# An RWKV block with routed experts on one core: the stages of time and channel mixing interleaved by batch

## The chip, the core and the metric

The kernel runs on one core of a Trainium2 chip, in fp32 throughout. Its time is the device time of one execution in microseconds (us); the figure that counts is the median of the runs shown. Five engines work side by side, each through its own list of instructions in a fixed order: TensorE (PE in the profile, with its weight loads PEld beside it), VectorE (DVE), ScalarE (ACT), GpSimd (POOL) and SyncE (SP), which issues the DMAs.

## The reference, cut to what matters

Four batches of 512 tokens with 512 channels pass through a modulated layer norm, a time mix, a channel mix, and then a block of two shared and sixteen routed experts (two of them for each token). Only the first part of it is touched. Cut down, with `h` the modulated layer norm of `x`:

```python
h1 = layer_norm(h, ln1_g, ln1_b); hh = time_shift(h1)     # one token back
k = (h1*tm_mk + hh*(1-tm_mk)) @ Wk.T                      # v and r alike
e2 = exp(tm_first + k - p); e1 = exp(-1e38 - p)           # p = max(-1e38, tm_first + k)
wkv = (e1*0 + e2*v) / (e1*0 + e2)
h = h + sigmoid(r) * wkv @ Wo.T                           # time mix
h2 = layer_norm(h, ln2_g, ln2_b); hh = time_shift(h2)
kk = (h2*cm_mk + hh*(1-cm_mk)) @ Wkey.T                   # 512 -> 2048
sr = sigmoid((h2*cm_mr + hh*(1-cm_mr)) @ Wcr.T)
h = h + sr * (silu(kk) @ Wval.T)                          # channel mix, 2048 -> 512
x = x + ga * h                                            # then the experts
```

Nothing passes from one batch to another before the experts, so the batches may be worked off in any order. The experts need the router's picks of all batches: the rows of each expert are counted batch by batch.

## The kernel before, in words

**Stages.** The work is a row of stages, one batch in each: T0 T1 T2 T3 (time mixes of batches 0 to 3), then C0 C1 C2 C3 (channel mixes), then the shared and routed experts. T0 (`time_first`, L402) starts the kernel and is of its own form.

**Time mix** (`time_mix`, L455). For each of four blocks of 128 output channels, m = 0 to 3, TensorE makes a k product, a v product and an r product (`k_step` L371, `v_step` L379, `r_step` L387), each a group of four 128x512 matmuls in `project` (L320). Behind each, VectorE, ScalarE and GpSimd work: after k the tiles p, e1, e2 (`exponents`, L338); after v the sum and the numerator av (`fraction`, L350); after r an exponential (`gated`, L358). What is left of a block, `divide` (L363), is put off: it is kept in a list `pend`, and `flush` (L334) issues it, at the next k or v step, or ahead of the output products. `divide` is one two-input VectorE operation, a reciprocal, and a GpSimd product that gives the finished gated tile. `o_steps(b)` (L393) flushes, then makes the output product of the time mix for each of four token tiles, four matmuls each (the last of the four needs the gated tile of m = 3), and VectorE adds the result onto the residual `x1s[b]`. In T2 and T3 the output products of the batch before are issued behind m = 0.

**Channel mix** (`channel_mix`, L577). First four products cr, one for each token tile (L596 to L614), with four sets of two subtractions on VectorE beside them (`key_terms`, L588; T1, T3, T2, T4 in the program's names). In C0 the output products of T3 stand behind the second cr. Then the key phase: four pairs of blocks, each with seven products of 128x256 matmuls (a Strassen form on 2x2 blocks; the banks are kx, ky and kz, and VectorE and ScalarE turn them into the tiles a11, a12, a21, a22; `ku` at L675 is VectorE's sum that releases ky's bank for its second use). Then the value phase: seven products in two halves each (`product`, L696; banks x, y, z), between which VectorE forms differences of the a tiles (`minus`, L720) and adds results to the residual (`result`, L723).

Strassen needs sums of weight blocks. Those for the keys are made in C0 by VectorE (`key_sums`, L504) and stored to DRAM for the later stages (`keep_keys`, L511). Those for the values (`value_sums`, L531) are made in T3: eight loads of quarters, sixteen subtractions of 128x512 on VectorE in four sets, and sixteen stores.

**What is woven in.** Each stage is a generator that yields behind each group of products, and at each yield `weave` (L1213) takes one step of a second generator, `back`. A list `plan` can say otherwise for each yield (0 or 1 steps):

```python
for _ in main:
    for _ in range(next(plan, 1)):
        next(back, None)
```

What is left of `back` when the stage's products are all issued is then drained. The back generators are the layer norms and the mixes ahead of a later stage, and the router behind an earlier one:

- `time_front(b)` (L272): statistics, modulation, statistics again, normed rows (ScalarE), then transposes on TensorE and the mixes for k, v and r. A statistics is `bn_stats`, `bn_aggr` and a small add on VectorE and a power on GpSimd; a modulation is two operations on VectorE.
- `channel_front(b)` (L305): statistics, normed rows, transposes, two mixes.
- `channel_back(b)` (L801): statistics, a modulated tile `h3r`, transposes, then the router: logits, the two picks, counts, and 8 small matmuls `ps_rows` at the end.

Before, T1 carries `time_front(2)`, T2 `time_front(3)`, T3 `front_and_sums` (L565: `channel_front(0)` with `value_sums` in its odd steps); C1 carries `channel_front(2)` and then `channel_back(0)`, C2 `channel_front(3)` and then `channel_back(1)`, C3 `channel_back(2)`; C0 carries `channel_front(1)`.

**Order and buffers.** The order of instructions on each engine is the order in which the program issues them (L66); no scheduler moves them. An instruction that must wait holds up all that stand behind it on its engine. All loads and stores of this part are issued on SP's queue, in the same way. Weights live in `wpool`: eight buffers of 1 MB, taken in turn, so that a load waits for the last reader of the tile that had its buffer (L72, L88). The time weights wk, wv, wr, wo are loaded once at the start (L113, L115); wcr and the first keys at T3 (L1273, L1274); then two tiles of keys for each pair (`load_keys`, L485) and seven tiles of values (`get`, L618) in each C stage. Rows of tokens live in 65 tiles of 128x512, and there are four `ps` and four `acc` banks of PSUM.

Of the kernel before, what the change touches and what calls it, by code (L numbers as in the profile page):

```python
# [44 lines left out]
def adaln_block(  # L45
# [274 lines left out]
    def project(w, acts, m, ps):  # L320

        for k in range(NK):
            nc.tensor.matmul(ps, w[:, k, m * P : (m + 1) * P], acts[k], start=(k == 0), stop=(k == NK - 1))  # L323

    def project_tokens(w, acts, t, ps):

        for k in range(NK):
            nc.tensor.matmul(ps, acts[k][:, t * P : (t + 1) * P], w[:, k, :], start=(k == 0), stop=(k == NK - 1))  # L328


    rws = [None] * B
    pend = []

# [36 lines left out]

    def k_step(b, m):  # L371
        ps = bank(f"ps_k_{b}_{m}")
        project(wk, time_mixes[b][MK], m, ps)
        yield
        out = exponents(b, m, ps)
        flush()
        return out

    def v_step(b, m, st, tag="ps"):  # L379
        ps = bank(f"ps_v_{b}_{m}", tag)  # L380
        project(wv, time_mixes[b][MV], m, ps)
        yield
        out = fraction(b, m, ps, *st)
        flush()
        return out

    def r_step(b, m, st):  # L387
        ps = bank(f"ps_r_{b}_{m}")
        project(wr, time_mixes[b][MR], m, ps)
        yield  # L390
        gated(b, m, ps, *st)

    def o_steps(b):  # L393
        flush()
        for t in range(NT):
            ps = bank(f"ps_o_{b}_{t}", "acc")
            project_tokens(wo, rws[b], t, ps)
            yield
            nc.vector.tensor_add(x1s[b][t], x1s[b][t], ps)
        rws[b] = None  # L400
# [53 lines left out]

    def time_mix(b):  # L455
        rws[b] = []
        if 1 < b < B - 1:
            time_loads(b + 1)
        for m in range(NK):
            st = yield from k_step(b, m)  # L460
            st = yield from v_step(b, m, st)
            yield from r_step(b, m, st)
            if m == 0 and b > 1:
                yield from o_steps(b - 1)
        time_mixes[b] = None


    h3_d = dram.tile([N, H], F32, tag="h3_d", name="h3_d")
# [33 lines left out]
    loaded = {}  # L502
# [28 lines left out]
    def value_sums():  # L531


        def load(n):
            t = [row_tile(f"wsum_{n}_{q}", (P, 2, HT)) for q in range(4)]
            for q in range(4):
                i, j = divmod(q, 2)
                at = i * (FF // 2) + n * 2 * P
                rows = wval_t[at : at + 2 * P, j * HT : (j + 1) * HT]
                nc.sync.dma_start(t[q], rows.rearrange("(k p) o -> p k o", p=P))  # L540
            return t

        def store(n, t):
            at = slice(n * 2 * HT, (n + 1) * 2 * HT)
            for i, q in ((T1, Q11), (T3, Q12), (T2, Q22), (T4, Q21)):
                nc.sync.dma_start(sums_d[i - T1, :, at].rearrange("p (k o) -> p k o", k=2), t[q])

        ahead = [load(0), load(1)]
        done = None
        yield  # L550
        for n in range(N_PAIR):
            t = ahead.pop(0)
            nc.vector.tensor_sub(t[Q11], t[Q12], t[Q11])
            nc.vector.tensor_sub(t[Q12], t[Q22], t[Q12])
# [10 lines left out]
    def front_and_sums():  # L565

        sums = value_sums()
        next(sums)
        for i, _ in enumerate(channel_front(0, "acc")):
            if i % 2:  # L570
                next(sums, None)
            yield
        yield from sums

    gas = {}

    def channel_mix(b):  # L577
# [18 lines left out]
        for t in range(NT):  # L596
            ps = bank(f"ps_cr_{b}_{t}")
            project_tokens(wcr, xr, t, ps)
            yield
            sr = row_tile(f"sr_{b}_{t}")  # L600
            nc.scalar.activation(sr, ps, AF.Sigmoid)
            nc.gpsimd.tensor_mul(sr, sr, ga)
            srs.append(sr)
            if b == 0 and t == 1:
                yield from o_steps(B - 1)
                key_sums(0)
            key_terms(t)
# [148 lines left out]
        result(2, HT, c5)  # L756

        if b + 1 < B:
            load_keys(b + 1, 0)
            gas[b + 1] = spread(GA, b + 1)  # L760
        yield from product(Q22, a12, Z, False)
        nc.vector.tensor_add(u2, u2, Z)
        result(0, HT, u2)

        yield from product(T4, a22, Y, False)
        nc.vector.tensor_add(c1, c1, Y)
        result(2, 0, c1)
# [445 lines left out]
    def weave(main, back, plan=()):  # L1213

        plan = iter(plan)
# [4 lines that stand above are left out]
    def drain(back):  # L1220
        for _ in back:
            pass

    def chained(*parts):
        for p in parts:
            yield from p()
# [39 lines left out]
        next(back)  # L1266
    weave(first, back, (1, 1, 1, 1, 0, 0, 0))
    drain(back)
    for b in range(1, B):
        if b + 1 < B:  # L1270
            back = chained(lambda: time_front(b + 1))
        else:
            wcr = load_w(wcr_t, "wcr")  # L1273
            loaded[0] = load_keys(0, 0)  # L1274
            back = front_and_sums()
            gas[0] = spread(GA, 0)
        weave(time_mix(b), back)
        drain(back)
    nc.sync.dma_start(router[:, :, :E_RT], w_router.rearrange("(k p) e -> p k e", p=P))
    for b in range(B):  # L1280
        parts = []
        if b + 1 < B:
            parts.append(lambda: channel_front(b + 1, "ps"))
        if b >= 1:
            parts.append(lambda: channel_back(b - 1))
        back = chained(*parts)

        plan = {0: [1] * 6 + [0] * 14, B - 1: [1] * 4 + [0, 0, 1] * 4}
        weave(channel_mix(b), back, plan.get(b, ()))
        drain(back)  # L1290
        if b == 0:
            clear_rest()
    shared = [load_shared(e) for e in range(E_SH)]
    gbs = [spread(GB, b) for b in range(B)]
    mids = [None] * B
# [87 lines left out]
```

## Time and profile before

| | |
|---|---|
| median of 3 runs | 1048.02 us (1046.33 to 1049.45) |
| the profiled execution, on its own clock | 1048.66 us |
| span of its trace | 1046.9 us |
| mean granted TensorE clock | 0.991 |
| start and end of T1 on TensorE | 96.74 to 139.69 us |
| T2 | to 205.15 us |
| T3 | to 267.19 us |
| C0, C1, C2 | to 394.73, 513.44 and 632.76 us |
| moved by DMA | 182.8 MB |

The span is what the trace covers; the execution's time is 1.8 us longer. Busy times count the instructions of an engine; weight loads (PEld) run beside the matmuls. In a line of a timeline the first number is the start in us of the span, the second the length, then engine, source line, operation, output and inputs by the program's names, and in brackets how long the engine was idle ahead of it and which instruction ended that wait.

### The profile page before, as it was taken

Reading aid. Unit: us, or ns where it says so; the run is one execution under the profiler, and the core shown is the slowest. Engines: PE = TensorE matmul, PEld = TensorE weight load, DVE = VectorE, ACT = ScalarE, POOL = GpSimd, SP = SyncE. Lnnn points to the kernel's source line nnn. Section 1 sums busy time; section 2 is a strip of 40 time slices with the busy share of each in tenths; the row PEclk is TensorE's granted clock in tenths of the full one; section 3 lists DMA queues with packets and bytes.
Section 4 is the critical chain, followed back from the end, with each engine's and each line's share of the span. In section 5 each row is a group of like instructions: output and inputs, shape, how many; then the busy total and the mean of one; then the engine's idle time right before and its main releaser. Section 6 shows DMA issues by size and latency. Waiting matters only on the chain. (4 is left out here: it accounts for less than half of the span.)

```text
span 1046.9 us, 11349 instructions
## 1 busy us (share of the span) xinstructions
PE 1013.1 (97%) x3824; PEld 667.1 (64%) x3824; DVE 637.5 (61%) x1174; ACT 302.2 (29%) x490; POOL 341.4 (33%) x322
## 2 busy tenths in 40 slices
PE   7998989989999999999999999999998999999997
PEld 2443434434478886888788886888745666566643
DVE  5887998897756535665757487447646322234427
ACT  1744452624323402621143102230030222122210
POOL 2453463532463007330164006420004222041250
PEclk9999989999999999999999999999999999999999
DMA  9700130443047761356332814642443999899853
GB/s 322 242 1 2 40 101 0 131 139 125 19 173 270 280 241 66 106 204 228 111 101 75 296 41 170 239 164 81 151 152 110 326 382 383 287 331 319 283 178 114
DMA packets 96619, 182.80 MB, mean 175 GB/s; under 512 B 7512, under 2 KB 50008, under 8 KB 92464
## 3 DMA queue, kind: packets, MB, share of 16 engines
q1 hardware_dynamic: 90720, 162.92, 45.0%
q0 software_dynamic: 5840, 19.14, 5.7%
q8 instruction: 31, 0.51, 0.2%
q14 instruction: 28, 0.23, 0.1%
HBM read 149.75 MB, written 32.29 MB: 174 GB/s over the span
## 5 line engine op out<-in xcount | busy, mean ns | idle before, releaser
L202 POOL TENSOR_TENSOR rstd_ln<-rstd_ln,minus_half 128x1 f32<-128x1 f32 x64 | 42.5, 664 | 192.0 <-DVE rstd_ln L201 179.5
L705 PE MATMUL ps_y<-wval,a 128*128 128x256 f32 x384 | 85.7, 380 | 0.0
L1112 POOL DMA_INDIRECT xg<-h_d,token x41 | 39.0, 950 | 126.0 <-PE ps_down L1151 41.1
L1151 PE MATMUL ps_down<-wrt,at 128*128 128x512 f32 x164 | 77.3, 593 | 1.7 <-issue 1.7
L705 PEld LDWEIGHTS ps_y<-wval,a 128*128 128x128 f32 x384 | 72.3, 190 | 9.5
L1135 PE MATMUL ps_up<-wrt,xt 128*128 128x256 f32 x328 | 77.8, 380 | 0.1
L246 DVE SCALAR_TENSOR_TENSOR mix_ln<-hT_ln,inv,mix_ln 128x511 f32<-128x511 f32 x64 | 56.4, 924 | 17.5 <-ACT mix_ln L240 16.8
L1135 PEld LDWEIGHTS ps_up<-wrt,xt 128*128 128x128 f32 x328 | 59.1, 190 | 7.5 <-DVE xt L1129 1.1
L634 PE MATMUL ps_ky<-T,keys_hi 128*128 128x256 f32 x256 | 60.9, 381 | 2.4 <-DVE ku L675 1.3
L1129 DVE COPY xt<-ps_xt 128x512 f32<-128x512 f32 x41 | 28.3, 689 | 55.8 <-PE ps_xt L1127 42.3
L328 PE MATMUL ps_o<-wo,av 128*128 128x512 f32 x128 | 57.9, 604 | 4.2 <-POOL av L366 4.0
L634 PE MATMUL ps_kx<-mix_ln,keys_lo 128*128 128x256 f32 x256 | 60.5, 379 | 0.0
L323 PE MATMUL ps_v<-mix_ln,wv 128*128 128x512 f32 x128 | 58.8, 603 | 0.0
L323 PE MATMUL ps_r<-mix_ln,wr 128*128 128x512 f32 x128 | 57.6, 593 | 0.1
L705 PE MATMUL ps_x<-wval,a 128*128 128x256 f32 x256 | 57.4, 380 | 0.0
L705 PE MATMUL ps_z<-wval,a 128*128 128x256 f32 x256 | 57.3, 380 | 0.0
L1057 PE MATMUL ps_up_sh<-h,wsh 128*128 128x512 f32 x128 | 57.2, 593 | 0.0
L1071 PE MATMUL ps_down_sh<-wsh,mid 128*128 128x512 f32 x128 | 56.3, 594 | 0.3 <-PEq L1325 0.3
L328 PE MATMUL ps_cr<-wcr,mix_ln 128*128 128x512 f32 x128 | 55.7, 592 | 0.0
L634 PEld LDWEIGHTS ps_ky<-T,keys_hi 128*128 128x128 f32 x256 | 47.9, 190 | 10.5 <-DVE ku L675 2.4
L222 ACT ACTIVATE xn_ln<-x,nm_ln,rstd_ln 128x512 f32<-128x512 f32 x32 | 25.8, 812 | 99.6 <-DVE nm_ln L215 99.5
L365 DVE RECIPROCAL p<-p 128x512 f32<-128x512 f32 x16 | 53.6, 3353 | 0.6
(223 smaller groups left out, 1834.9 us busy)
## 6 DMA issues: line engine op xcount, KB each, us to landing
wrt<-in_rt_up_dram SPq DMA_DIRECT2D x41, 512.0 KB
wrt<-in_rt_down_dram SPq DMA_DIRECT2D x41, 512.0 KB
wval<-sums_d SPq DMA_DIRECT2D x16, 1024.0 KB
wval<-in_wval_t_dram SPq DMA_DIRECT2D x12, 1024.0 KB
keys_lo<-keys_d SPq DMA_DIRECT2D x12, 1024.0 KB
y_d<-y SPq DMA_DIRECT2D x41, 256.0 KB
keys_hi<-keys_d SPq DMA_DIRECT2D x12, 768.0 KB
mod<-mod_d SPq DMA_DIRECT2D x22, 256.0 KB
```

The lines of the kernel that those rows point to most:

```text
L202: nc.gpsimd.tensor_tensor(rstd, rstd, minus_half, ALU.pow)
L246: nc.vector.scalar_tensor_tensor(t[:, 1:], hT[:, : T - 1], inv[:, m - MK, k : k + 1], t[:, 1:], ALU.mult, ALU.add)
L323: nc.tensor.matmul(ps, w[:, k, m * P : (m + 1) * P], acts[k], start=(k == 0), stop=(k == NK - 1))
L328: nc.tensor.matmul(ps, acts[k][:, t * P : (t + 1) * P], w[:, k, :], start=(k == 0), stop=(k == NK - 1))
L365: nc.vector.reciprocal(p, p)
L634: nc.tensor.matmul(ps[:, c * HT : (c + 1) * HT], w[:, k, c * P : (c + 1) * P], acts[k], start=(fresh and c == 0 and k == 0), stop=(c == 1 ...
L705: nc.tensor.matmul(ps[:, j * HT : (j + 1) * HT], acts[p][:, c, j * P : (j + 1) * P], w[:, i, :], start=(fresh and i == 0 and j == 0), stop ...
L1057: nc.tensor.matmul(ps, wu[:, k, m * P : (m + 1) * P], h3s[b][k], start=(k == 0), stop=(k == NK - 1))
L1071: nc.tensor.matmul(ps, mids[b][j][:, t * P : (t + 1) * P], shared[j // ND][1][:, j % ND, :], start=(j == 0), stop=(j == len(mids[b]) - 1),)
L1112: nc.gpsimd.indirect_dma_start(out=xg, out_offset=None, in_=h3_d, in_offset=bass.IndirectOffsetOnAxis(ap=token[:, s : s + 1], axis=0),)
L1135: nc.tensor.matmul(ps[:, :D], xt[:, k, :], wu[:, k, :], start=(k == 0), stop=(k == NK - 1))
L1151: nc.tensor.matmul(ps, at[:, j, :], wd[:, j, :], start=(j == 0), stop=(j == ND - 1))
```

## The change

The stages are put in the order T0 T1 C0 T2 C1 T3 C2 C3. What follows from that, and is part of it:

- The back generators move. T1, T2 and T3 now carry `channel_front(0)`, `channel_front(1)` and `channel_front(2)`. C0 carries the rest of `value_sums` and then `time_front(2)`; C1 `time_front(3)` and then `channel_back(0)`; C2 `channel_back(1)` and then `channel_front(3)`; C3 `channel_back(2)`. `front_and_sums` is gone; the first loads of `value_sums` are issued behind T1, its sixteen subtractions in C0's first yields.
- The output products of batch b+1 are issued in C(b), behind its second cr product, for b = 0, 1, 2. T2 and T3 have none any more.
- The time weights lose their buffers to keys and values, and are loaded again: wk, wv and wr late in C0 and C1 (ahead of the value products Q22 and T4), wo in T2 and T3 behind m = 0. That is eight loads of 1 MB more. The first keys of C1 and C2 are loaded behind m = 2 of T2 and T3, and no longer late in C0 and C1.
- wcr and the first keys are loaded ahead of T1, the rows of batch 3 (`time_loads(3)`) behind C0.

The number of matmuls and of operations on the data is the same.

```diff
+    tw = dict(k=wk, v=wv, r=wr, o=wo)
+    tw_next = {}
+
+    def load_time(*names):
+        for n in names:
+            tw_next[n] = load_w(dict(k=wk_t, v=wv_t, r=wr_t, o=wo_t)[n], f"w{n}")
...
     def time_mix(b):
         rws[b] = []
-        if 1 < b < B - 1:
-            time_loads(b + 1)
+        tw.update(tw_next)
+        tw_next.clear()
         for m in range(NK):
             st = yield from k_step(b, m)
             st = yield from v_step(b, m, st)
             yield from r_step(b, m, st)
-            if m == 0 and b > 1:
-                yield from o_steps(b - 1)
+            if b > 1:
+                if m == 0:
+                    load_time("o")
+                elif m == 2:
+                    load_keys(b - 1, 0)
         time_mixes[b] = None
+        tw.update(tw_next)
+        tw_next.clear()
...
     def channel_mix(b):
...
             srs.append(sr)
+            if b + 1 < B and t == 1:
+                yield from o_steps(b + 1)
             if b == 0 and t == 1:
-                yield from o_steps(B - 1)
                 key_sums(0)
             key_terms(t)
...
         if b + 1 < B:
+            gas[b + 1] = spread(GA, b + 1)
+        if b < B - 2:
+            load_time("k", "v")
+        elif b + 1 < B:
             load_keys(b + 1, 0)
-            gas[b + 1] = spread(GA, b + 1)
         yield from product(Q22, a12, Z, False)
...
+        if b < B - 2:
+            load_time("r")
         yield from product(T4, a22, Y, False)
...
-    for b in range(1, B):
-        if b + 1 < B:
-            back = chained(lambda: time_front(b + 1))
-        else:
-            wcr = load_w(wcr_t, "wcr")
-            loaded[0] = load_keys(0, 0)
-            back = front_and_sums()
-            gas[0] = spread(GA, 0)
-        weave(time_mix(b), back)
-        drain(back)
+    wcr = load_w(wcr_t, "wcr")
+    loaded[0] = load_keys(0, 0)
+    back = channel_front(0, "acc")
+    gas[0] = spread(GA, 0)
+    weave(time_mix(1), back)
+    drain(back)
+    vsums = value_sums()
+    next(vsums)
...
+    parts = {
+        0: [lambda: vsums, lambda: time_front(2)],
+        1: [lambda: time_front(3), lambda: channel_back(0)],
+        2: [lambda: channel_back(1), lambda: channel_front(3, "ps")],
+        3: [lambda: channel_back(2)],
+    }
+    plan = {0: [1] * 6 + [0] * 14, B - 1: [1] * 4 + [0, 0, 1] * 4}
     for b in range(B):
-        parts = []
-        if b + 1 < B:
-            parts.append(lambda: channel_front(b + 1, "ps"))
-        if b >= 1:
-            parts.append(lambda: channel_back(b - 1))
-        back = chained(*parts)
-
-        plan = {0: [1] * 6 + [0] * 14, B - 1: [1] * 4 + [0, 0, 1] * 4}
+        back = chained(*parts[b])
         weave(channel_mix(b), back, plan.get(b, ()))
         drain(back)
         if b == 0:
             clear_rest()
+        if b < B - 2:
+            if b == 0:
+                time_loads(3)
+            back = channel_front(b + 1, "acc")
+            weave(time_mix(b + 2), back)
+            drain(back)
```

In `k_step`, `v_step`, `r_step` and `o_steps` the names wk, wv, wr, wo become `tw["k"]`, `tw["v"]`, `tw["r"]`, `tw["o"]`.

More of the change, by code (lines that the diff above doesn't have):

```diff
@@ L372, in k_step @@
         ps = bank(f"ps_k_{b}_{m}")
-        project(wk, time_mixes[b][MK], m, ps)
+        project(tw["k"], time_mixes[b][MK], m, ps)
         yield
@@ L380, in v_step @@
         ps = bank(f"ps_v_{b}_{m}", tag)
-        project(wv, time_mixes[b][MV], m, ps)
+        project(tw["v"], time_mixes[b][MV], m, ps)
         yield
@@ L388, in r_step @@
         ps = bank(f"ps_r_{b}_{m}")
-        project(wr, time_mixes[b][MR], m, ps)
+        project(tw["r"], time_mixes[b][MR], m, ps)
         yield
@@ L396, in o_steps @@
             ps = bank(f"ps_o_{b}_{t}", "acc")
-            project_tokens(wo, rws[b], t, ps)
+            project_tokens(tw["o"], rws[b], t, ps)
             yield
@@ L563, in value_sums @@
         store(*done)
[L565 to L573, printed above, removed]
     gas = {}
```

## The prediction

> **What bounds the kernel now.** I read the page first. TensorE is the one engine that is nearly always busy:
>
> ```profile
> PE 1013.1 (97%) x3824; PEld 667.1 (64%) x3824; DVE 637.5 (61%) x1174; ACT 302.2 (29%) x490; POOL 341.4 (33%) x322
> ...
> PE   7998989989999999999999999999998999999997
> ```
>
> The change adds and removes no matmul, so it can win only what TensorE loses, and where it loses is read stage by stage. In the view by windows, T1, T2, T3 and C0:
>
> ```profile
> 96.74:139.69 42.95, 42.95 (x113) 19.79 (x112) 40.08 (x56) 18.10 (x29) 18.71 (x17) 1.00 0.24 67
> 139.69:205.15 65.46, 59.96 (x147) 26.45 (x146) 58.46 (x75) 32.48 (x51) 33.65 (x27) 0.95 0.20 64
> 205.15:267.19 62.04, 58.80 (x146) 26.35 (x145) 52.93 (x67) 21.02 (x32) 20.30 (x17) 0.97 0.37 121
> 267.19:394.73 127.54, 126.81 (x529) 98.49 (x528) 69.67 (x108) 31.68 (x48) 40.68 (x34) 1.00 0.56 198
> ```
>
> Columns: length, then PE, PEld, DVE, ACT, POOL busy, PE clock, DMA share, GB/s. In the T stages VectorE is 85 to 93% full, in C0 55%. TensorE's timeline shows what that does at the start of T2 and, behind the transposes of channel_front(0), at m = 1 of T3:
>
> ```profile
> 139.69 1.92 PE L323 MATMUL ps_k<-mix_ln,wk 128*128 128x512 f32 x4
> 143.84 1.21 PE L323 MATMUL ps_k<-mix_ln,wk 128*128 128x512 f32 x2 [2.23 <-DVE mix_ln L246]
> 147.20 2.08 PE L323 MATMUL ps_k<-mix_ln,wk 128*128 128x512 f32 x2 [2.14 <-DVE mix_ln L246]
> ...
> 233.27 5.29 PE L323 MATMUL ps_k<-mix_ln,wk 128*128 128x512 f32 x8
> ```
>
> An undisturbed group of four matmuls 512 wide goes every 3.43 us (96.74, 100.17, 103.61 in the timeline), a block of o or cr takes 13.73, a set of four transposes 0.44. From 96.74 to 267.19 that makes 36x3.43 + 2x13.73 + 12x0.44 = 156.3 of 170.45: **14.1 us lost in T1 to T3**, none in T1, 8.8 in T2 and 5.4 in T3 (the same count, with the windows' lengths). C0, C1 and C2 lose 1.6, 1.3 and 1.9 by the same count.
>
> **What goes.** time_front (25 us of VectorE: eight statistics of 1.02, four modulations of 1.5 to 2.3, eight mixes of 0.70 to 1.57) leaves T1 and T2; channel_front (13 us) comes. T1 ran with the heavier load and lost nothing, so I cost the new T1, T2 and T3 at no loss: -14.1. Also replaced: the late o product in C0 (0.8), a wait of 0.64 in each of C1 and C2, 0.5 at ps_rows in C2: -2.6. Together **-16.7**.
>
> **What comes: o_steps behind two cr products.** o of batch b+1 needs its last gated tile, which needs the reciprocal of m=3. `flush()` now stands behind the back steps of cr 0 and cr 1. How that chain runs, C0 shows (VectorE, GpSimd, TensorE):
>
> ```profile
> 267.51 2.86 DVE L594 TENSOR_TENSOR T<-mix_ln 128x256 f32<-128x256 f32 x2
> ...
> 271.37 0.68 DVE L364 SCALAR_TENSOR_TENSOR p<-er,p 128x512 f32<-128x512 f32 x1
> 272.08 3.35 DVE L365 RECIPROCAL p<-p 128x512 f32<-128x512 f32 x1
> ```
> ```profile
> 276.15 1.26 POOL L366 TENSOR_TENSOR av<-av,p 128x512 f32<-128x512 f32 x1
> ```
> ```profile
> 274.05 2.74 PE L328 MATMUL ps_o<-wo,av 128*128 128x512 f32 x6
> 277.47 11.43 PE L328 MATMUL ps_o<-wo,av 128*128 128x512 f32 x26 [0.68 <-POOL av L366]
> ```
>
> TensorE needs the tile 9.4 us after the last r product (two cr, 6.87, and three matmuls of o, 2.57); from the reciprocal's end to it go 1.4 (GpSimd 1.26 and hand-over). VectorE's tail of T ends about 1.3 after the last r (from the end of k of m=2, 18.9 before it: p and e 1.5, divide 4.1, mixes, av, mixes, mixes bound by ScalarE to 12.3; p and e 1.4, divide 4.1, mixes 1.85, av 0.65). Then, in the built order, ahead of the divide (4.1):
> - C0: value_sums twice, 3.6 + 4.2 (the rows: 2.8 alone, 3.7 with GpSimd busy), T1 0.75: 1.3+3.6+0.75+4.2+4.1+1.4 = 15.3, **5.9 late**.
> - C1: two statistics 2.0, T1 0.75, a modulation with statistics 3.0 (2.64 at 101.83): 12.5, **3.1 late**.
> - C2: statistics, T1, statistics, h3r: 1.0+0.75+1.0+1.9: 11.4, **2.0 late**.
>
> All of TensorE queues behind that matmul. In the old order a whole m of T (10.3) lay between. Bounds: uncontended and with T's tail on time 3, 1 and 0; every two-input operation at its contended row (T 2.86, sums 3.7, modulation 4.1) 9, 8 and 6. I take the middle, since GpSimd is busy about half of these stretches.
>
> **The clock** makes a gap dearer. After these gaps the windows show:
>
> ```profile
> 147.00:150.00 3.00, 2.80 (x4) 1.26 (x5) 2.93 (x6) 0.20 (x1) 3.00 (x3) 0.50 0.00 0
> 233.00:236.00 3.00, 2.90 (x5) 1.36 (x6) 2.90 (x5) 2.17 (x4) 0.00 (x0) 0.58 0.64 231
> ```
>
> The group at 233.27, behind a gap of 2.94, took 5.13 to the next start in place of 3.43: 1.7 more. Gaps of 1.1 and 0.68 show nothing. I add 1.7 for C0 and C1 and half for C2's 2.0: **4.2**. The Trainium skill ("TensorE: Matmul & The Clock Gate", section "What's actually happening") says that the clock halves after an idle window of about 3.4 us and that the window runs free. By it, the gaps of 3.1 and 2.0 here could pass unpunished and the sum would be 2.5 us lower; here gaps of 2.2 to 2.9 already halved it, so the rows decide.
>
> **C0's value phase.** time_front(2) gets its 7th step before VectorE subtracts a11 for the product T2. Before, the first subtraction ended 3.5 after the late key product, when TensorE came (348.08 to 352.41 with a transpose set). Now a modulation with statistics, 2.64, goes ahead: 2.7 late; two more statistics before the third subtraction: 1.6 more. **4.4** with the clock (half speed hides in the second wait); 2.5 to 6.1 as bounds.
>
> **C2's key phase.** channel_back(1) now leads the chain, so the router falls among key products, which hand banks to VectorE every few us. Before, it fell in the value phase, whose sums wait longer:
>
> ```profile
> 613.24 0.78 DVE L921 TENSOR_TENSOR sums<-sums,ps_n 128x16 f32<-128x16 f32 x4
> ...
> 620.91 1.11 DVE L972 TENSOR_SCALAR at_row<-ramp,row_of,number 128x128 f32<-128x128 f32 x4
> ```
>
> That block is 8.7 long. Counted from kx of pair 1, it can start at 18.7 (a12 and a21 of pair 1 before it) and ends at 27.4; TensorE is at ps_rows at 21.2. The eight ps_rows (1.7) then trickle, and ky waits for ku (0.65): 5.3 late, plus 1.7 clock: **7.0** (5 to 9). The other router block (3.7) ends at 11.9 against 12.1, just in time. The two table loads more (13 against 11 in the built order, 1.28 each; one by C2's keys) end before VectorE is free.
>
> **Small ones.** time_front's four k steps in C1 put 3.6 of ScalarE each (0.77 + 3x0.71 + 0.71) among the copies of the key sums, in place of channel_front's 2.2, and a statistics and h3r go before ku: 2.0 (0 to 5). Statistics ahead of the same subtraction in C2's value phase: 1.3. Together **3.3**.
>
> **At nothing.** Eight loads more, 8 MB. wk and wv are issued when the first value products free their buffers, 41 us ahead of use; wr and wo later, each tens of us ahead. What stands before them on SP's queue (spread, zero stores, x of batch 3) has long been free. Without that cover 1 MB at the 322 GB/s of the first slice is 3.3 each, 26 for all. keys for C1 and C2 now start in m=2 of T, 38 ahead. The sums' stores precede keys of pair 1 on SP: issued some 20 after T1's end, used 22 later. GpSimd gets no work.
>
> **Sum:** 11.0 + 4.2 + 4.4 + 7.0 + 3.3 = 29.9 added, 16.7 gone: +13.2. The profiled execution took 1048.66 (span 1046.9), 0.64 above the median: 1061.9 on its scale, **1061** as a median.
>
> **Rivals.**
> - VectorE reaches the divides in time (for: 45% idle in C0, the tail of T may end earlier; against: queue order). It decides at 8.0 us after the last r: a reciprocal that ends by then costs no o product. Then 15 of the first two terms go: 1046 to 1047, **not slower**. If the key and value waits also halve, 1041.
> - Contention throughout: o late by 9, 8, 6 with 5 clock, others at their upper ends: +28, **1076**.
> - Reloads or the key loads behind the sums' stores exposed: up to 26 more, 1085. The SP order speaks against it.
> - The T stages keep part of their loss (say 5), because it was not time_front: 1066. T1's zero speaks against.
>
> **Chances:** forecast (1055 to 1069) 0.57, in time 0.18, contention 0.17, exposed loads 0.03, T loss kept 0.05. About 0.3% is what a measurement can tell from no change. Of the second case two fifths are faster by more: faster 0.07, same 0.11, slower 0.82. The range is 1049 to 1077.
>
> **What would show it.** T2 and T3 without gaps at ps_k; gaps before the fourth o matmul in C0, C1, C2, released by GpSimd's av, near 6, 3, 2; a gap at C0's ps_y for a11; one at ps_rows in C2, near 4. Wrong if the o gaps are absent, if a reload or a key load releases TensorE, or if T2 starts late.

## The result, and the profile after

The changed kernel takes 1073.46 us (median of 4 runs, 1071.4 to 1075.57), the kernel before 1048.74 beside it (4 runs): a ratio of **1.0239, 95% interval 1.0209 to 1.0269**. The profiled execution took 1072.13 (span 1070.4, clock 0.979): 23.5 us of span more. The forecast was +13, so the direction was right, the time lies inside the range, and the size was too small by nearly half.

The page's line of engines and TensorE's row of slices, after:

```profile
PE 1022.8 (96%) x3824; PEld 673.8 (63%) x3824; DVE 641.9 (60%) x1174; ACT 305.1 (29%) x492; POOL 339.9 (32%) x322
...
PE   7998979999998999999897999999999999999997
```

TensorE's busy time grew by 9.7 (slow matmuls count as busy); the other 14 are idle. In the row, slices of 26.8 us each, the dips behind 134, 321, 508 and 562 us (7, 8, 8, 7) are new. Where they belong, the view by windows tells: T1, C0, T2, C1, T3, C2 of the changed kernel (length; PE, PEld, DVE, ACT, POOL busy; clock; DMA share; GB/s):

```profile
97.14:140.10 42.96, 42.96 (x114) 19.80 (x113) 32.34 (x42) 20.21 (x31) 14.34 (x14) 1.00 0.31 101
140.10:283.67 143.57, 130.71 (x529) 99.78 (x528) 102.99 (x147) 37.91 (x57) 51.78 (x42) 0.96 0.58 203
283.67:326.63 42.96, 42.96 (x113) 19.80 (x112) 33.89 (x46) 20.27 (x31) 13.97 (x13) 1.00 0.47 165
326.63:466.45 139.82, 134.81 (x578) 104.12 (x576) 92.84 (x195) 39.45 (x63) 51.80 (x45) 0.98 0.37 131
466.45:509.40 42.95, 42.95 (x113) 19.80 (x112) 33.95 (x46) 20.20 (x31) 13.96 (x13) 1.00 0.14 37
509.40:657.21 147.81, 138.29 (x577) 106.76 (x576) 82.17 (x181) 36.45 (x56) 42.94 (x37) 0.95 0.34 120
```

The reader is to see two things. Every T stage takes 42.95, its undisturbed length (12 groups of 3.43 and four sets of transposes), with VectorE at 75 to 79%: the 14 us that T2 and T3 lost before are won. And the C stages now lose far more than that. Counted with the undisturbed lengths of cr and o blocks, key and value products, transposes and the router's matmuls (C0 125.95; C1 and C2 131.1, the o block included), C0 loses **17.6**, C1 **8.7**, C2 **16.7**: 43.0, where the whole stretch lost 18.9 before. The difference, 24.1, is the result; the span grew by 23.5, since 0.4 more is lost ahead of T1 and 1.0 less behind C2.

TensorE's timeline shows where. Its lines with a wait of over 1.1 us in C0, C1 and C2, and the slow products behind the last of them:

```profile
157.61 13.02 PE L328 MATMUL ps_o<-wo,av 128*128 128x512 f32 x26 [7.91 <-POOL av L373]
...
181.21 1.12 PE L637 MATMUL ps_ky<-T,keys_lo 128*128 128x256 f32 x2 [1.98 <-DVE T L596]
...
240.40 7.14 PE L708 MATMUL ps_y<-wval,a 128*128 128x256 f32 x32 [2.62 <-issue]
...
340.55 13.71 PE L328 MATMUL ps_o<-wo,av 128*128 128x512 f32 x26 [4.31 <-POOL av L373]
...
521.94 13.12 PE L328 MATMUL ps_o<-wo,av 128*128 128x512 f32 x26 [2.93 <-POOL av L373]
...
582.65 3.65 PE L988 MATMUL ps_rows<-at_slot,at_row 128*128 128x47 f32 x16 [5.21 <-DVE at_row L980]
586.08 3.76 PE L637 MATMUL ps_ky<-T,keys_hi 128*128 128x256 f32 x8
589.64 2.54 PE L637 MATMUL ps_kz<-mix_ln,keys_hi 128*128 128x256 f32 x8
```

The first, fourth and fifth are the output products, each released by GpSimd's `av` at L373, as forecast, but after 7.9, 4.3 and 2.9 us in place of 5.9, 3.1 and 2.0. The second is the first key product of C0 that needs the tile T2: a wait that the forecast did not have. The third is the value product y of C0, the last three the router's `ps_rows` in C2 and two key products behind it, which take 3.6 and 2.4 in place of 1.73 because the clock is down.

### The profile page after: what moved, and what is told of

Same layout as the page of the kernel before. It is cut to its first block, busy times and chain, and to the rows that moved or that the text cites. A ratio compares the mean times of both kernels' runs of the same rounds, so it can differ in the third digit from the quotient of the medians.

```text
span 1070.4 us, 11384 instructions
## 1 busy us (share of the span) xinstructions
PE 1022.8 (96%) x3824; PEld 673.8 (63%) x3824; DVE 641.9 (60%) x1174; ACT 305.1 (29%) x492; POOL 339.9 (32%) x322
## 5 line engine op out<-in xcount | busy, mean ns | idle before, releaser
L708 PEld LDWEIGHTS ps_y<-wval,a 128*128 128x128 f32 x384 | 73.5, 193 | 15.3 <-issue 3.0
L328 PE MATMUL ps_o<-wo,av 128*128 128x512 f32 x128 | 62.7, 644 | 18.4 <-POOL av L373 17.5
L328 PEld LDWEIGHTS ps_o<-wo,av 128*128 128x128 f32 x128 | 25.9, 207 | 52.7 <-issue 30.5
```

The source lines that it names most:

```text
L708: nc.tensor.matmul(ps[:, j * HT : (j + 1) * HT], acts[p][:, c, j * P : (j + 1) * P], w[:, i, :], start=(fresh and i == 0 and j == 0), stop ...
```

## The experiments

All ratios are to the kernel before on the same chip; "faster" and "slower" are differences of medians, against the changed kernel's 1073.46 unless said otherwise.

**1. The divide first.** One line at the head of `channel_mix`:

```diff
+        flush()
         for t in range(NT):
             ps = bank(f"ps_cr_{b}_{t}")
```

> One line more than the changed kernel: the put-off divide of m=3 is issued at the head of each channel mix, ahead of the back steps of the first two cr products. Theory Q (VectorE's queue, and VectorE full in C0): the o waits of 7.9, 4.3 and 2.9 us go, and with them the slow matmuls behind them (o blocks 9.8, 6.9 and 4.9 us longer than an undisturbed 13.73). In C1 and C2 that is won, 11 to 12 us. In C0 it isn't: VectorE is busy 42.5 of the first 44.9 us, its work ends no earlier, and the wait comes back at the first ky product for the tile T2, 10 to 13 us long in place of 4.3; C0 wins 0 to 3. Total 12 to 15 faster than the changed kernel, about 1060. Rival O (only the order of the divide counts, as my prediction had it): 21.6 faster, about 1052. Rival C (the divide is late wherever it stands, because the tail of the T stage and GpSimd are late): at most 3 faster, 1070 or more.

Measured: 1064.46, ratio 1.0155 (1.0134 to 1.0176): 9 faster, less than the 12 to 15 that were expected. The o waits are gone in all three stages. But in C0 the time came back at the first ky product:

```profile
179.25 1.22 PE L638 MATMUL ps_ky<-T,keys_lo 128*128 128x256 f32 x2 [9.74 <-DVE T L596]
```

C0 went from 143.57 to 141.65, C1 only from 139.82 to 137.42 (new waits of 1.83 and 1.33 at its key products), C2 from 147.81 to 143.70. Rival O, which is how the prediction summed, and rival C fall. In C0 the order of the divide hardly matters. Theory Q's reason, a VectorE that is full, is only a part of it. The first key sum and the last T sets on VectorE:

```profile
169.31 0.68 DVE L518 TENSOR_TENSOR keys_lo<-keys_hi 128x512 f32<-128x512 f32 x1
...
177.72 5.69 DVE L596 TENSOR_TENSOR T<-mix_ln,T 128x256 f32<-128x256 f32 x4
```

From 169.31 to 183.41 key sums and T sets took 14.1, beside products of GpSimd; alone they take 4.6 (experiments 7 and 11), and the first T set that ky needs is then ready 3.6 behind the start of the key sums. An estimate from these rows: alone, ky would have waited some 3.5, so about 6 of the 9.7 come from the work beside GpSimd and not from the order. The changed kernel's 42.5 busy of VectorE's first 44.9 us hold the same slow stretch. C1 won less than theory Q had it too: the second of its new waits stands behind two of time_front(3)'s mixes, the first behind a product of GpSimd for which VectorE waited.

**2. The value sums in T1.**

```diff
-    back = channel_front(0, "acc")
+    back = front_and_sums()
...
-        0: [lambda: vsums, lambda: time_front(2)],
+        0: [lambda: time_front(2)],
...
-    plan = {0: [1] * 6 + [0] * 14, B - 1: [1] * 4 + [0, 0, 1] * 4}
+    plan = {0: [0] * 4 + [1] * 2 + [0] * 14, B - 1: [1] * 4 + [0, 0, 1] * 4}
```

`front_and_sums` is that of the kernel before; the plan keeps time_front(2) at its yields.

> The value sums' sixteen subtractions stand in T1, in the odd steps of channel_front(0), as they stood in T3 before; C0 keeps time_front(2) at the same yields. Theory Q: VectorE has 12 us less in C0's first 45: the o wait of 7.9 falls under 1 and the wait of 4.3 at the first ky product under 1.5; C0 wins 12 to 14. T1, whose VectorE is busy 32.3 of 43.0, becomes full and loses 2 to 6 (T3 of the kernel before lost 5.4 with the same work and an o addition more). Total 7 to 12 faster than the changed kernel, 1061 to 1066. Rival G (the ky wait comes from GpSimd's queue, where a power for time_front(2) holds the residual's products back until they fall on the key sums): the o wait goes, the ky wait of about 4 stays; total 3 to 7 faster.

Measured: 1072.54, ratio 1.0240 (1.0209 to 1.0270): 1 faster, which is nothing, where theory Q had 7 to 12 and rival G 3 to 7. The trace shows why; TensorE in C0:

```profile
147.75 6.61 PE L328 MATMUL ps_cr<-wcr,mix_ln 128*128 128x512 f32 x10 [5.04 <-DVE mix_ln L246]
...
157.61 11.43 PE L328 MATMUL ps_o<-wo,av 128*128 128x512 f32 x26 [0.68 <-POOL av L373]
...
179.61 0.70 PE L647 MATMUL ps_ky<-T,keys_lo 128*128 128x256 f32 x2 [1.98 <-DVE T L606]
```

The o wait fell to 0.68, as theory Q said. But T1's VectorE (40.2 of 43.0 busy) was now late with the mixes for cr, and the first cr block took 14.2 in place of 6.9. And the ky wait stayed at 1.98, though VectorE had been idle 7 us shortly before. On that point rival G was right and theory Q wrong.

**3. C2's back generators exchanged.**

```diff
-        2: [lambda: channel_back(1), lambda: channel_front(3, "ps")],
+        2: [lambda: channel_front(3, "ps"), lambda: channel_back(1)],
...
-    plan = {0: [1] * 6 + [0] * 14, B - 1: [1] * 4 + [0, 0, 1] * 4}
+    plan = {0: [1] * 6 + [0] * 14, 2: [0] * 4, B - 1: [1] * 4 + [0, 0, 1] * 4}
```

> C2's two back generators change places (channel_front(3) first, four yields later, then channel_back(1)), so that the router's block falls among the value products, as in the kernel before; nothing is left out. Theory Q: C2's o wait of 2.9 goes too, since only a T set stands ahead of the divide (4.9 with the slow matmuls), the wait of 5.2 at ps_rows goes with the 4 us of slow matmuls behind it (9.3), and 0.6 to 1.2 come back at ku and ps_rows as in the kernel before. Total 12 to 14 faster, about 1060. Rival: the router's block makes TensorE wait wherever it stands, since VectorE needs 8.7 us for it: 5 faster (the o wait alone). All other stages as in the changed kernel.

Measured: 1060.12, ratio 1.0105 (1.0073 to 1.0137): 13.3 faster. C2 took 134.05. The router block does not make TensorE wait wherever it stands: among the key products it cost 9.7, among the value products no wait is left that it ends (C2 loses 2.9 in all, 0.74 of it at o and 0.64 at ku).

**4. No reloads.**

```diff
-            tw_next[n] = load_w(dict(k=wk_t, v=wv_t, r=wr_t, o=wo_t)[n], f"w{n}")
+            tw_next[n] = wcr
```

> The eight reloads of time weights are left out: T2 and T3 use wcr in place of wk, wv, wr and wo, so their products are others and so may be the router's picks. Read up to the end of C2 only, and by TensorE's waits. My theory (the reloads cost nothing): C3 begins within 0.7 us of the changed kernel's 657.2, with the same waits at o, ky, y and ps_rows. Rival (the eight loads take time from the keys and values on SP's queue): C3 begins 3 to 20 us earlier, and waits released by loads disappear.

Measured: from the start of T2 to C3, 372.8 in place of 373.5, with the same waits at o (4.31, 2.93), ps_rows (5.21) and y (1.04). C0, ahead of it, took 146.6, with its waits unchanged and more slow matmuls behind them (see the last section); experiment 3, which has all its loads, took 146.5. C3 therefore began at 660.6, not 657.2, which is more than the 0.7 that was expected at most. The whole time (1075.7, one run) says nothing more, since the products of T2 and T3 are others. The reloads cost nothing that TensorE sees; in the changed kernel wk is issued at 237.8, lands 7.3 later and is used at 283.7.

**5. time_front(2) later in C0.**

```diff
-    plan = {0: [1] * 6 + [0] * 14, B - 1: [1] * 4 + [0, 0, 1] * 4}
+    plan = {0: [1] * 4 + [0] * 8 + [1] * 7 + [0] * 3, B - 1: [1] * 4 + [0, 0, 1] * 4}
```

> Only C0's plan is changed: time_front(2)'s first seven steps stand at yields 13 to 19 (among the key products) instead of beside the last o products and the first value products; value_sums stays where it is. Theory G (C0's wait at the first ky product comes from GpSimd's queue: the powers of time_front(2) hold the residual's products back until they run beside the key sums and the T sets, which then take twice their time): the o wait stays at 7.9, the ky wait of 2.3 (4.3 us with what follows) goes to under 0.5, the wait of 2.6 at y goes too, and the steps cost 0 to 2 among the key products: 4 to 7 faster than the changed kernel, 1066 to 1069. Rival Q (VectorE is simply full there): the ky wait stays over 1.5, since only 5 us of VectorE's work leave that stretch and its end is set by the sums and the o additions: 1 to 3 faster, all of it at y.

Measured: 1077.53, ratio 1.0285 (1.0257 to 1.0313): 4 slower by the medians, where 4 to 7 faster was expected; the intervals of the two ratios overlap, but in the trace C0 takes 148.9 in place of 143.6. Both waits that theory G named are gone (first ky, y), and the o wait stayed at 7.89, but four new ones stand among the key products (1.64, 2.65, 3.24, 2.60), each ended by VectorE. G named the cause and I mis-sized the price: key products hand a bank to VectorE every 1.7 us, and a modulation with its statistics (2.6) ahead of `ku` or of key sums does not fit.

**6 and 7. Combinations.** The divide first (as in 1), C2 exchanged (3), time_front(3) paused at two yields of C1, time_front(2) as in 5; in 7, two of the four sets of value sums in T1 as well. The plan of 6, and what 7 adds:

```diff
+    plan = {0: [1] * 4 + [0] * 8 + [1] * 7 + [0] * 3, 1: [1] * 4 + [0] * 2, 2: [0] * 4, B - 1: [1] * 4 + [0, 0, 1] * 4}
```
```diff
+    def front_and_sums(sums):
+        next(sums)
+        for i, _ in enumerate(channel_front(0, "acc")):
+            if i in (1, 3):
+                next(sums)
+            yield
...
+    plan = {0: [0] * 2 + [1] * 2 + [0] * 8 + [1] * 7 + [0] * 3, 1: [1] * 4 + [0] * 2, 2: [0] * 4, B - 1: [1] * 4 + [0, 0, 1] * 4}
```

> The changed order with four repairs: the divide of m=3 at the head of each channel mix, time_front(2) later in C0 (as in the run before), time_front(3) paused for the last two o yields of C1, and C2's back generators exchanged. No work is left out. Expected from the runs so far: no o wait over 0.7 in any stage; C0 2 to 5 late at the first ky product (four sets of value sums, 12.8, and four additions, 2.8, behind a divide that ends 6.6 after the stage's start, against 21 until the key sums must begin), so C0 wins 12 to 15; C1 4 to 6; C2 13 to 14. Total 30 to 34 faster than the changed kernel: 1040 to 1044, below the kernel before by 5 to 9. If VectorE's queue alone were the bound wherever the work is put, C0 and C1 would win under 5 together: about 1055.

Measured: 1055.77, ratio 1.0074 (1.0054 to 1.0094). C1 and C2 take 133.7 and 133.1, C0 takes 148.8: the first ky product waits 7.88, and the four waits of experiment 5 are there. No power holds GpSimd's residual work back here. But with the o block on time the key sums fall beside GpSimd's work for the last two cr products, and with the T sets they take 11.5 (165.33 to 176.86) in place of 4.6; by the same estimate as in experiment 1, ky would have waited about 1 without that. Worse than expected by 12 and more, all of it in C0.

> As the run before, and two of the four sets of value sums stand in T1, at the second and the fourth step of channel_front(0); two stay in C0, at the third and fourth yield. Theory Q: T1's VectorE has 10.6 us to spare and takes 6 to 8, so T1 and the first cr product lose 0 to 2 (with all four sets there they lost 7.3); C0's ky wait falls under 1. 2 to 4 faster than the run before: 1037 to 1041. Rival: any set in T1 delays the mixes for cr as four did, half of 7.3: no gain against the run before.

Measured: 1044.54, ratio **0.9970 (0.9957 to 0.9982)**: below the kernel before, and 11 faster than 6, where 2 to 4 was expected. T1 took the two sets free of charge (42.95, VectorE 37.9 busy), no o and no first ky wait is left (key sums and T sets took 4.6, from 161.46 on, and GpSimd was idle beside them until 164.96); what remains are the four waits among C0's key products:

```profile
195.39 1.97 PE L646 MATMUL ps_ky<-T,keys_lo 128*128 128x256 f32 x8 [1.65 <-DVE keys_lo L519]
...
203.45 3.57 PE L646 MATMUL ps_ky<-T,keys_hi 128*128 128x256 f32 x8 [2.65 <-DVE ku L687]
...
213.87 1.97 PE L646 MATMUL ps_ky<-T,keys_lo 128*128 128x256 f32 x8 [1.66 <-DVE keys_lo L519]
...
221.89 1.99 PE L646 MATMUL ps_ky<-T,keys_hi 128*128 128x256 f32 x8 [2.60 <-DVE ku L687]
```

**8. One part of the change alone, in the old order:** value_sums from T3 to C0.

```diff
-            back = front_and_sums()
+            back = channel_front(0, "acc")
...
+    vsums = value_sums()
+    next(vsums)
...
-        parts = []
+        parts = [lambda: vsums] if b == 0 else []
...
-        plan = {0: [1] * 6 + [0] * 14, B - 1: [1] * 4 + [0, 0, 1] * 4}
+        plan = {0: [1] * 10 + [0] * 10, B - 1: [1] * 4 + [0, 0, 1] * 4}
```

> The kernel before, its stage order kept, with one part of the change alone: value_sums goes from T3 to C0's first four yields, ahead of channel_front(1)'s steps. Theory Q: T3 gets back its loss (5.4 us by the count of undisturbed groups), and C0's o product waits 6 to 8 in place of 0.7, with 1.7 to 2.5 of slow matmuls behind it, and 2 to 4 at the first ky product: 4 to 9 slower than the kernel before, 1053 to 1058. That is about half of the changed kernel's loss, without any change of the order. Rival (the loss comes from the interleaved order itself, where no T stage lies between the divide and the output products): within 1 of T3's gain, 1043 to 1046.

Measured: 1055.01, ratio 1.0070 (1.0048 to 1.0092), 8 above the kernel before. T3 took 56.70, its undisturbed length, in place of 62.04. C0 took 137.77 in place of 127.54, with

```profile
279.86 13.18 PE L328 MATMUL ps_o<-wo,av 128*128 128x512 f32 x26 [6.45 <-POOL av L366]
```

So both the gain in T3 and the loss at C0's o product come from where the sums stand, with the old order of stages untouched; rival "order" falls for C0's o product. The 2 to 4 expected at the first ky product did not come.

**9 and 10. C0's front spread out.** All of 7, but time_front(2)'s first two steps stand at C0's first yields, ahead of the sums; the next two at yields 16 and 19 (9) or 19 and 20 (10); the rest from 23 on. What changes in C0, and its plan in 9 and in 10 (which also has a yield between the two lines that end the generator):

```diff
+    def sums_and_front():
+        front = time_front(2)
+        for _ in range(2):
+            next(front)
+            yield
+        yield from vsums
+        yield from front
...
+    plan = {0: [1] * 4 + [0] * 11 + [1, 0, 0, 1] + [0] * 3, 1: [1] * 4 + [0] * 2, 2: [0] * 4, B - 1: [1] * 4 + [0, 0, 1] * 4}
...
+    plan = {0: [1] * 5 + [0] * 13 + [1, 1] + [0] * 2, 1: [1] * 4 + [0] * 2, 2: [0] * 4, B - 1: [1] * 4 + [0, 0, 1] * 4}
```

> The version with two sets of value sums in T1, and in C0 the steps of time_front(2) put elsewhere: its first two (statistics, one modulation) ahead of the two sets of sums at the first two yields, the next at yields 16 and 19 (the second yield of the third and the fourth pair of key products), the rest from yield 23 on, behind the first value products. Theory Q: what decides is whether VectorE's work of a step fits behind the products that follow it. The four waits of 1.6 to 2.7 in the key phase (8.6 us, with slow matmuls 11.4 of C0's 137.4) came from modulations ahead of ku and key sums; at a second yield a step costs 0 to 1.5. C0 loses 1 to 5 in place of 11.4: 7 to 10 faster than that version, 1035 to 1038. Rival (GpSimd's queue again: the powers of the first two steps hold the residual's products back until the key sums): 2 to 4 come back at the first ky product, 1038 to 1041.

Measured: 1045.00, ratio 0.9947 (0.9929 to 0.9965): level with 7 by the medians, 2 us faster by the ratios, where 7 to 10 was expected. One wait is left in the key phase (0.97 for key sums), and 3.71 stand at the first ky product.

> As the run before, with the two middle steps of time_front(2) both in the last pair (yields 19 and 20), where no key sums are made, and the last store of the value sums at yield 5. Theory Q: no step of the front stands beside key sums any more, so the key phase loses under 1; the statistics at yield 20 may cost up to 1 at y. C0 loses 0.5 to 3: 1034 to 1037, 0 to 2 faster than the run before.

Measured: 1044.02, ratio **0.9935 (0.9918 to 0.9951)**, the lowest ratio of all, though its interval overlaps that of 9. The key phase is clean, as theory Q said, but here too the wait at the first ky product came back, which the rival of 9 had named:

```profile
174.13 1.18 PE L646 MATMUL ps_ky<-T,keys_lo 128*128 128x256 f32 x2 [3.71 <-DVE T L604]
```

So C0 takes 133.66 where 126.5 to 129 was expected. The version of 7, with its waits in the key phase, takes 137.43 there. The 3.8 between them agree with the ratios (0.35% of 1048 is 3.7); the medians, taken on different chips, differ by 0.5 only. In the two traces, 1.0 of the difference is lost again ahead of T1 and 2.0 behind C2, where the kernels are the same. VectorE's work ahead of the key sums (the first two steps, 5.4 in this trace, and two sets of sums) has its part in this wait: its key sums began 3.5 after the last o product, in 7 at 0.8. So they fell beside GpSimd's products for the last two cr, which run from 165.97 to 178.01, and with the T sets they took 13.2.

**11 and 12. GpSimd's residual work moved.** Two operations behind each pair of key products instead of beside the cr products, in the changed kernel (11) and in the version of 10 (12):

```diff
-                nc.gpsimd.tensor_mul(x1[t - 1], x1[t - 1], ga)
-                nc.gpsimd.tensor_add(x1[t - 1], x1[t - 1], xres[t - 1])
...
                 keep_keys(p)
+            nc.gpsimd.tensor_mul(x1[p], x1[p], ga)
+            nc.gpsimd.tensor_add(x1[p], x1[p], xres[p])
```

> The changed kernel with one thing moved: GpSimd's eight operations on the residual (times the gate, plus the row of x; 1.3 us each) stand behind the four pairs of key products, two behind each, and no longer beside the cr products. Theory G (in C0 VectorE's key sums and T sets take twice their time because GpSimd works beside them: 14.2 us from the first key sum to the last T, against 4.8 in the kernel before): with GpSimd idle there they take 5 to 8, the wait at the first ky product (4.3 with what follows) goes, and the o wait stays at 7.9: 3 to 5 faster than the changed kernel. Rival (they are slow for another reason, such as the transfers of that stretch): the ky wait stays over 1.5, at most 1 faster.

Measured: 1082.96, ratio 1.0352 (1.0326 to 1.0378): 9.5 slower, the wrong sign. Yet the mechanism is there. VectorE from the first key sum to the T sets, first in the changed kernel, then in this one:

```profile
171.28 1.71 DVE L518 TENSOR_TENSOR keys_lo<-keys_hi 128x512 f32<-128x512 f32 x1
173.02 1.64 DVE L519 TENSOR_TENSOR keys_lo<-keys_lo 128x512 f32<-128x512 f32 x1
174.58 0.68 DVE L520 TENSOR_TENSOR keys_hi<-keys_lo,keys_hi 128x512 f32<-128x512 f32 x1
175.19 1.75 DVE L521 TENSOR_TENSOR keys_hi<-keys_lo 128x512 f32<-128x512 f32 x1
176.86 2.89 DVE L596 TENSOR_TENSOR T<-mix_ln,mix_ln 128x256 f32<-128x256 f32 x2
179.68 5.69 DVE L596 TENSOR_TENSOR T<-mix_ln,T 128x256 f32<-128x256 f32 x4
```
```profile
172.00 0.68 DVE L518 TENSOR_TENSOR keys_lo<-keys_hi 128x512 f32<-128x512 f32 x1
172.72 0.69 DVE L519 TENSOR_TENSOR keys_lo<-keys_lo 128x512 f32<-128x512 f32 x1
173.33 0.68 DVE L520 TENSOR_TENSOR keys_hi<-keys_lo,keys_hi 128x512 f32<-128x512 f32 x1
173.93 0.68 DVE L521 TENSOR_TENSOR keys_hi<-keys_lo 128x512 f32<-128x512 f32 x1
174.54 0.75 DVE L596 TENSOR_TENSOR T<-mix_ln,mix_ln 128x256 f32<-128x256 f32 x2
175.21 1.42 DVE L596 TENSOR_TENSOR T<-mix_ln,T 128x256 f32<-128x256 f32 x4
```

The same six groups take 14.1 in the one and 4.6 in the other, and the first ky wait is gone. What was gained there is paid several times over among the pairs: the moved operations run beside the key sums of the next pair, which then take 6.0 in place of 3.9, and `ku` is late by 2.1 again and again, in C1 too:

```profile
199.67 3.60 PE L632 MATMUL ps_ky<-T,keys_hi 128*128 128x256 f32 x8 [2.15 <-DVE ku L673]
...
216.02 2.89 PE L632 MATMUL ps_ky<-T,keys_hi 128*128 128x256 f32 x8 [2.09 <-DVE ku L673]
```

> The fastest version so far (front at yields 19 and 20, two sets of value sums in T1) with GpSimd's residual work moved in the same way. Theory G: its wait of 3.7 at the first ky product in C0 (with the slow matmuls behind it 5 to 6) goes; the key sums of the later pairs may be slowed by up to 1. C0 falls from 133.7 to 127 to 129: 4 to 7 faster than that version, about 0.988 of the kernel before. Rival as in the run before: no gain.

Measured: 1051.94, ratio 1.0042 (1.0024 to 1.0060): slower than the version of 10 by 8 (medians) to 11 us (ratios), where 4 to 7 faster was expected, in the same way; its first ky wait is gone (key sums and T sets took 5.7), and `ku` waits 2.1 three times in C0, 3.1 in C1.

## Why the prediction was wrong in size

Point by point, the forecast and what the changed kernel's trace has (each loss with the slow matmuls behind it):

| step of the prediction | forecast | measured |
|---|---|---|
| T1 to T3 lose nothing any more | -14.1 | -14.1 |
| o late in C0, C1, C2, with the clock (11.0 + 4.2) | 15.2 | 9.8 + 6.9 + 4.9 = 21.6 |
| C0's first ky product | none | 4.3 |
| C0's value phase, y | 4.4 | 2.8 |
| C2's key phase, router | 7.0 | 9.7 |
| small ones (C1 key, C2 value) | 3.3 | 2.0 |
| reloads, key loads, table loads | 0 | 0 |

What was added sums to 40.4, forecast 29.9. With the 10.5 between them the forecast of +13.2 becomes +23.7; the spans differ by 23.5. So the terms are complete to within 0.4 or so, and three steps failed.

**The step "o_steps behind two cr products"** had the right queue and the right order of the three stages, and was mis-sized. C0's chain on VectorE, and GpSimd's hand-over:

```profile
142.03 1.16 DVE L565 TENSOR_TENSOR wsum<-wsum,wsum 128x512 f32<-128x512 f32 x1
...
146.23 1.82 DVE L596 TENSOR_TENSOR T<-mix_ln 128x256 f32<-128x256 f32 x2
147.98 1.75 DVE L565 TENSOR_TENSOR wsum<-wsum,wsum 128x512 f32<-128x512 f32 x1
...
151.82 0.68 DVE L371 SCALAR_TENSOR_TENSOR p<-er,p 128x512 f32<-128x512 f32 x1
152.54 3.35 DVE L372 RECIPROCAL p<-p 128x512 f32<-128x512 f32 x1
```
```profile
156.04 1.52 POOL L373 TENSOR_TENSOR av<-av,p 128x512 f32<-128x512 f32 x1 [6.86 <-DVE p L372]
```

T's tail ended 1.9 after the last r product, not 1.3; the two sets of sums took 4.2 and 3.8 (forecast 3.6 and 4.2), T1 1.8 (0.75), the divide 4.0, GpSimd's product and its hand-over 1.7 (1.4): 17.5 after the last r product, in place of 15.3. In C1 and C2 the same small misses, and a modulation whose second half took 1.58, make 1.2 and 0.9 more. The clock's part was 6.4, not 4.2: C2's gap of 2.9 was paid in full, and C1's with 2.6. I had announced the middle between uncontended and contended rows, but had put T1 and GpSimd's product into the sum at their uncontended 0.75 and 1.26; they took 1.75 and 1.52.

**The step that was missing** is C0's first ky product. I had followed the divide to the o product and stopped there. Behind the o block come the key sums and the T sets, which C0 of the kernel before did in 4.6 us (289.54 to 294.16) while GpSimd stood still until 293.04. The first and the last of them there:

```profile
289.54 0.68 DVE L506 TENSOR_TENSOR keys_lo<-keys_hi 128x512 f32<-128x512 f32 x1
...
292.74 1.42 DVE L594 TENSOR_TENSOR T<-mix_ln,T 128x256 f32<-128x256 f32 x4
```

Now a power of time_front(2) stands in GpSimd's queue ahead of the residual's first product and waits for VectorE's statistics:

```profile
170.66 0.55 POOL L202 TENSOR_TENSOR rstd_ln<-rstd_ln,minus_half 128x1 f32<-128x1 f32 x1 [3.52 <-DVE rstd_ln L201]
171.18 1.26 POOL L614 TENSOR_TENSOR x<-x,mod 128x512 f32<-128x512 f32 x1
172.52 1.59 POOL L615 TENSOR_TENSOR x<-x,xr 128x512 f32<-128x512 f32 x1
```

That product, which nothing else held back since 157.6, starts at 171.18, a tenth of a us before the first key sum, and GpSimd then works through the whole stretch. Experiment 5 took the power away, 11 the products: both times the wait went. What decides most of it is whether GpSimd works beside the key sums and T sets, whatever brings it there. Where they took 11.5 to 14.1 us (the changed kernel, 1 to 4, 6, 9 and 10), ky waited; where they took 4.6 to 5.7 (the kernel before, 5, 7, 11 and 12), it did not. In 6 there is no power, and the wait was 7.88. The prediction said that GpSimd gets no work, and that is true (322 instructions in both kernels); in the changed kernel its work was moved against VectorE's by a wait that the change put into its queue.

The Trainium skill ("SBUF — State Buffer", section "Who interferes with whom") says that VectorE and GpSimd share a pair of ports as an exclusive lock, that an operation of VectorE with two SBUF inputs contends with one of GpSimd that reads SBUF, and that the loser is blocked for a whole instruction. The trace agrees: a key sum takes 0.68 with GpSimd idle and 1.64 to 1.75 beside a GpSimd product of 1.3, and that product takes up to 1.7 itself.

**The step "C2's key phase"** had the place and the wait right: ps_rows waited 5.2, forecast 5.3 with its trickle and ku. The clock's part was mis-sized: 1.7 forecast, about 4 measured, since 8 small matmuls and two key products ran slow: the granted clock was 0.50, 0.50 and 0.62 in the three windows of 3 us behind the wait.

Against that, y in C0 cost 2.8, not 4.4: its first wait was 2.62 as forecast (2.7), the second did not come, and that the clock held behind the first was luck (see the last section). Of the rivals, "in time", "reloads exposed" and "T loss kept" fall. "Contention throughout" comes nearest by the time it states (1076), but its own terms (23 and 5, then 6.1, 9 and 6.3, less 16.7) add up to about 33 and not 28, which is 1081. Nor does it fit by its pieces: its o waits of 9, 8 and 6 were not reached, and the missing wait is not in it.

What the experiments leave of the change itself: the 14 us in T1 to T3 are won, but 5.4 of them are T3's and come with the value sums' leaving it, in the old order too (experiment 8). The other 8.8, T2's, come with the new order; no run shows whether the old one could win them by moving back work alone. With the back work put elsewhere C1 and C2 lose under 3 each (experiments 7 and 10). C0 keeps 7.7 even in the version of 10, where value sums, key sums, GpSimd's work and time_front(2) meet. A version with the first steps of time_front(2) behind the key phase as well, and two sets of sums in T1, was not tried.

## What to carry to other kernels

In a hand-ordered kernel, follow each late instruction past the first engine that waits for it: moving one instruction forward can move the wait and not remove it (here 7.9 at o became 9.7 at ky). Then ask why the engine is full: a part of its busy time can be operations made slower by a neighbour (key sums and T sets, 4.6 alone, took 14.1 beside GpSimd). Look for room by stretches of 10 us rather than by stage (T1 took two sets of sums for nothing and four for 7 us), and remember that an instruction that waits in one engine's queue can push harmless work behind it against a third engine's critical stretch.

## What the runs showed of the hardware that was not expected

The same wait can cost the clock or not. C0's y product waits 2.62 in six kernels. In the changed kernel and in experiments 1 and 11 the matmuls behind it ran at full clock, in experiments 2, 3 and 4 at half. Transfers don't decide it: in experiment 4, with a DMA share of 0.04 there, the clock was 0.51. Experiment 7 has both in one execution: its ky product behind a wait of 2.65 took 3.57, the one behind 2.60 took 1.99. The window of 3 us behind y's wait in the changed kernel, then in experiment 3 (the clock is the number behind the busy times):

```profile
240.40:243.40 3.00, 3.00 (x14) 2.66 (x15) 2.86 (x9) 0.59 (x2) 1.25 (x3) 1.00 0.93 343
```
```profile
242.56:245.56 3.00, 3.00 (x7) 2.46 (x8) 2.86 (x9) 0.59 (x2) 1.26 (x3) 0.52 0.97 363
```

The product took 7.14 in the one and 8.58 in the other. The Trainium skill ("TensorE: Matmul & The Clock Gate", section "What's actually happening") says that the clock is set by a window that runs free, and that for this reason the point of the warm-up varies with where in the window the first matmul falls. That the same gap costs the clock or not would fit this, if gaps fall into the window in the same way; no run shows the window. Its length of some 3.4 us doesn't fit as a bound on the gap, since gaps of 2.6 and 2.9 halved the clock here. So one such wait may cost 1.4 us more or not, with nothing changed around it; together with the same luck behind the o and ky waits this is why C0 took 143.6 in the changed kernel and 146.5 in experiment 3, which doesn't differ from it there.
